# Layer norm, S4 convolution and NF4 gated MLP: the first weight tile's codes loaded in two halves, and another written order of the first tiles

## The chip, the cores and the metric

The kernel runs on one core of a Trainium2 chip. The metric is the device time of one execution in microseconds (us); lower is better. The engines that matter here are TensorE (PE, matrix products and transposes), VectorE (DVE), ScalarE (ACT), GpSimd (POOL) and SyncE (SP), which only issues DMAs. ACT issues a few DMAs too.

## The reference

For tokens x (2048 rows of 512 values, single precision) it computes, with xn the layer norm of x:

```python
x + s4(xn) + down(silu(gate(xn)) * up(xn))
```

`s4` is a causal convolution along the 512 features with a kernel derived from a state-space model. `gate` and `up` map 512 to 1792 features, and `down` maps back. Their weights are stored as 4-bit codes (one integer in 0..15 for each weight) and one scale for each block of 64 weights: weight = table[code] * scale, with a table of 16 values. Decoding the codes is part of the work.

## The kernel before

The tokens are worked on in four blocks of 512 rows (block 0 to 3), each of which has four groups of 128 rows. The 1792 hidden features are worked on in 14 weight tiles of 128, and tile m has a gate part and an up part of 128 x 512 values each. For every tile and block PE multiplies the tile's weights with the block's transposed, normalised tokens; ACT applies silu to the gate product, DVE multiplies it with the up product, and the result goes to device memory. After all tiles come the products with the down weights. In between lie the convolution and the work that prepares its kernel.

Decoding a tile takes eight `bends` (line 264): ACT passes over the codes in place with a piecewise linear function, the first one reading the integers. Bend j reads what bend j - 1 wrote. A multiply by the scales on DVE follows (`mul`), and then, for all products except the first ones, the weights and the tokens are split into three parts each (`split`, `part_of`), so that one product in full precision becomes three passes over faster operands. The exception is `native`: weight tile 0 on blocks 0 and 1 is multiplied unsplit, in full precision (line 469).

For a block of tokens the steps are: `stats` for each row group j (mean and variance, DVE), `scale` for a pair of row groups (1/sqrt by POOL), `norm` for each row group (DVE), `turn` for a pair of row groups (8 transposes on PE, with the pair number 0 or 1), then `copy` (ACT copies the transposes out, blocks 0 and 1) or `h`, `l`, `e` (the three parts).

The order of the start is written out by hand in the string `HEAD`. Each word is a step, and each engine executes its instructions in the order in which the words issue them; a loop at the end of the head ties every instruction of ACT, DVE, PE, POOL and SP to the one before it on the same engine. What an engine executes therefore follows from the words that concern it; a word of ACT moved past a word of DVE alone changes nothing. The numbers in the words are:

- `bend.m.j.k.h`: weight tile m, bend j, k = 0 gate or 1 up, h = half of the 512 columns. Without k and h: both parts whole.
- `mul.m.k.h`, `w.m.part` (split of tile m's weights, part 0 on ACT, 1 and 2 on DVE)
- `stats.b.j`, `scale.b.pair`, `norm.b.j`, `turn.b.pair`, `copy.b.pair`: block b
- `native.k.b.j.c`: gate or up, block b, row pair j, column pair c (two matrix products)
- `pass.k.m.b.part`: one of the three passes, four matrix products
- `silu.m.b`, `gated.m.b` (DVE, and then a store by SP), `awake.n` (n transposes whose result nobody reads)

The loads are issued before the list: gate's codes of tile 0 by ACT (line 573), then by SP the four row groups of block 0 as four DMAs (line 576), up's codes and the scales of tile 0, blocks 1 and 2, tile 1, block 3 and tile 2. The semaphores of these DMAs are used in rotation, eight of them, so each DMA from the ninth on waits for the landing of the one eight before it.

In the old list ACT has 19 bends of tile 0, then `copy.0.0`, two bends, `copy.0.1`, and the remaining eleven bends. PE has `awake.43`, `turn.0.0`, `awake.6`, `turn.0.1`, and then the native products. After the list an automatic scheduler orders the rest.

Of the kernel before, what the change touches and what calls it, by code (L numbers as in the profile page):

```python
# [9 lines left out]
I32 = mybir.dt.int32  # L10
# [8 lines left out]
HD = 512  # L19
# [44 lines left out]


HEAD = """
awake.43 stats.0.0 bend.0.0.0.0 bend.0.0.0.1 bend.0.1.0.0 stats.0.1 bend.0.1.0.1
bend.0.2.0.0 stats.0.2 bend.0.2.0.1 scale.0.0 bend.0.3.0.0 bend.0.3.0.1 stats.0.3
bend.0.4.0.0 bend.0.5.0.0 norm.0.0 bend.0.4.0.1 scale.0.1 bend.0.6.0.0 norm.0.1 bend.0.5.0.1
bend.0.7.0.0 turn.0.0 awake.6 bend.0.0.1.0 mul.0.0.0 bend.0.6.0.1 norm.0.3 bend.0.1.1.0  # L70
bend.0.7.0.1 norm.0.2 bend.0.2.1.0 mul.0.0.1 copy.0.0 turn.0.1 stats.1.0 bend.0.3.1.0
native.0.0.0.0 stats.1.1 bend.0.0.1.1 copy.0.1 native.0.0.0.1 stats.1.2 scale.1.0
bend.0.4.1.0 native.0.0.1.0 stats.1.3 bend.0.1.1.1 bend.0.5.1.0 bend.0.2.1.1 norm.1.1
native.0.0.1.1 scale.1.1 bend.0.6.1.0 norm.1.0 bend.0.7.1.0 bend.0.3.1.1 turn.1.0 mul.0.1.0
bend.0.4.1.1 norm.1.2 bend.0.5.1.1 native.1.0.0.0 norm.1.3 bend.0.6.1.1 bend.0.7.1.1
native.1.0.1.0 copy.1.0 mul.0.1.1 stats.2.1 turn.1.1 silu.0.0 stats.2.0 native.1.0.0.1 w.0.0
stats.2.3 scale.2.0 native.1.0.1.1 copy.1.1 stats.2.2 native.1.1.0.0 bend.1.0 norm.2.0
scale.2.1 native.1.1.0.1 norm.2.1 bend.1.1 gated.0.0 turn.2.0 norm.2.3 native.0.1.0.0 h.2.0
norm.2.2 w.0.1 turn.2.1 bend.1.2 native.0.1.0.1 e.2.0 bend.1.3 native.1.1.1.0 l.2.0 h.2.1
native.0.1.1.0 bend.1.4 native.0.1.1.1 e.2.1 native.1.1.1.1 bend.1.5 l.2.1 pass.0.0.2.0  # L80
bend.1.6 w.0.2 pass.1.0.2.0 bend.1.7 pass.0.0.2.1 stats.3.1 silu.0.1 pass.1.0.2.1 mul.1
load.3.0 bend.2.0 pass.0.0.2.2 stats.3.0 w.1.0 pass.1.0.2.2 gated.0.1 scale.3.0 bend.2.1
pass.0.1.2.0 w.1.1 h.0 pass.1.1.2.0 stats.3.2 pass.1.1.2.1 w.1.2 bend.2.2 pass.0.1.2.1
stats.3.3 pass.0.1.0.0 silu.0.2 bend.2.3 l.0 scale.3.1 pass.1.1.2.2 h.1 pass.0.1.2.2
pass.1.1.0.0 norm.3.0 e.0 bend.3.0 pass.1.1.0.1 pass.0.1.1.0 bend.2.4 pass.0.1.0.1 norm.3.3
silu.1.2 gated.0.2 pass.0.1.0.2 bend.3.1 norm.3.2 pass.1.1.0.2 norm.3.1 bend.3.2 gated.1.2
turn.3.1 silu.1.0 l.1 turn.3.0 pass.1.1.1.0 h.3.0 gated.1.0 pass.0.1.1.1 h.3.1 l.3.0
pass.1.1.1.1 bend.2.5 pass.0.1.3.0 l.3.1 bend.2.6 pass.1.1.3.0 e.3.0 bend.3.3 pass.0.1.3.1
e.3.1 bend.3.4 pass.0.0.3.0 pass.0.0.3.1 bend.2.7 e.1 pass.1.1.3.1 bend.3.5 pass.0.1.3.2
bend.3.6 mul.2 pass.0.0.3.2 bend.3.7 pass.1.0.3.0 mul.3 pass.1.1.3.2 pass.0.1.1.2 silu.1.3  # L90
w.2.0 pass.1.0.3.1 silu.0.3 w.2.1 pass.1.1.1.2 pass.0.2.0.0 silu.1.1 w.2.2 w.3.0
pass.1.2.0.0 w.3.1 pass.0.2.0.1 pass.1.2.0.1 gated.1.3 pass.1.2.0.2 gated.1.1 w.3.2
pass.0.2.0.2 pass.1.0.3.2 silu.2.0 gated.2.0 gated.0.3
"""


# [1 line left out]
def layernorm_s4_nf4_glu_kernel(  # L98
# [19 lines left out]
    V, S, G, T = nc.vector, nc.scalar, nc.gpsimd, nc.tensor  # L118
# [119 lines left out]
    def load_q(pair):  # L238
        n = "".join(f"{kind}{m}" for kind, m in pair)
        q = work.tile([P, 2, 512], F32, tag="q", name=f"q_{n}", bufs=3)  # L240
        sc = work.tile([P, 2, 512], F32, tag="sc", name=f"sc_{n}")
        qs[pair] = (q, sc, n)

    def load_codes(pair, k, eng):
        kind, m = pair[k]
        eng.dma_start(qs[pair][0][:, k, :].bitcast(I32), SRC[kind][0][m])
# [11 lines left out]
    def load_weights(pair):  # L258
        load_q(pair)
        for k in range(2):  # L260
            load_codes(pair, k, nc.sync)
            load_scales(pair, k)
# [256 lines left out]
        nc.sync.dma_start(res_dram[tb], xr)  # L519


    ALL = slice(0, HD)
    HALVES = (slice(0, HD // 2), slice(HD // 2, HD))

    def down(tb, wd):

        if tb == NTB - 1:
            po = [bank2(f"po{tb}_{j}")[:, 0, :] for j in range(4)]
        else:
            pj = [bank2(f"po{tb}_{jj}") for jj in range(2)]  # L530
            po = [pj[j // 2][:, j % 2, :] for j in range(4)]
        xr = work.tile([P, 4, HD], F32, tag="xt", name=f"xo{tb}")
        nc.gpsimd.dma_start(xr, res_dram[tb])  # L533
        for p in range(NPR):
            hr = work.tile([P, 2, 512], F32, tag="q", name=f"hr{tb}_{p}", bufs=3)
            nc.sync.dma_start(hr, h_dram[tb][p])
            hp = work.tile([P, 3, 2, 512], F32R, tag="wp", name=f"hp{tb}_{p}", bufs=4)
            split([hp[:, i, :, :] for i in range(3)], hr)
            for j in range(4):
                for k in range(2):  # L540
                    for part in range(3):
                        T.matmul(  # L542
                            po[j], hp[:, part, k, bass.ts(j, P)], wd(p, part, k),
                            start=(p == 0 and k == 0 and part == 0),
                            stop=(p == NPR - 1 and k == 1 and part == 2),
                        )
                if p == NPR - 1 and tb == NTB - 1:

                    for i, cs in enumerate(HALVES if j == 3 else (ALL,)):
                        o = xr[:, j, cs]  # L550
                        V.scalar_tensor_tensor(o, po[j][:, cs], OUT, o, ALU.mult, ALU.add)  # L551
                        (nc.scalar if i else nc.sync).dma_start(out[bass.ts(4 * tb + j, P), cs], o)
        if tb < NTB - 1:
            for jj in range(2):
                o = xr[:, 2 * jj : 2 * jj + 2, :]
                V.scalar_tensor_tensor(o, pj[jj], OUT, o, ALU.mult, ALU.add)
                nc.sync.dma_start(rows(out, tb)[:, 2 * jj : 2 * jj + 2, :], o)

    gu = lambda m: (("g", m), ("u", m))
# [9 lines left out]
    wp, ps, hs = {}, {}, {}  # L569
    sp = nc.sync  # L570
    load_q(gu(0))
    w0 = qs[gu(0)][0]
    load_codes(gu(0), 0, S)
    silu_set = const.tile([P, 1], F32, tag="silu_set", name="silu_set")
    S.activation(silu_set, mhalf[:, 0:1], AF.Silu)
    load_x(0, 1)
# [123 lines left out]
    for i in range((6 * NPR + 3) // 4):  # L700
        wt = work.tile([P, 4, 512], F32R, tag="xp", name=f"wdt{i}", bufs=12)
        s = 4 * i
        while s < min(4 * i + 4, 6 * NPR):
            e = min(4 * i + 4, 6 * (s // 6 + 1))
# [80 lines left out]
```

## Time and profile before

| what | us |
|---|---|
| median of three runs | 514.54 (514.51 to 515.04) |
| the profiled execution's own time | 514.13 |
| its span (first to last instruction) | 512.4 |
| PE busy | 507.1 (99% of the span) |
| DVE busy, ACT busy | 261.3, 264.3 |
| POOL busy | 24.5 |
| data moved by DMA | 96.33 MB, mean 188 GB/s |

Busy time is added up over the instructions of an engine. In the rows of a stage, the numbers stand for PE, PE's weight loads, DVE, ACT and POOL in this order, each followed by its number of instructions, and then the granted clock of PE, the mean busy share of the DMA engines, and the rate in GB/s. A row of the timeline or of the chain of waits begins with its start in the span and its length. "L267" is line 267 of the kernel before. In the trace each full-precision product of 256 columns makes two rows.

### The profile page before, as it was taken

The numbers are of one execution on the slowest core, as the hardware profiler recorded it, in microseconds if no ns is written. First come the engines' busy times: TensorE is split into PE (matmuls) and PEld (weight loads), VectorE is DVE, ScalarE is ACT, GpSimd is POOL, SyncE is SP. The second block draws the span as 40 slices with busy tenths as digits, with TensorE's granted clock in tenths as the row PEclk, the third lists the DMA queues.
The fourth block names the chain that finished last, engine by engine and source line by source line (L and its number), as shares of the span: only waits on it lengthen the run. The fifth ranks groups of instructions, "written<-read, shape, count | busy, mean of one in ns | idle before, by whom it ended". The sixth has DMA issues, their size and how long they took to land.

```text
span 512.4 us, 6160 instructions
## 1 busy us (share of the span) xinstructions
PE 507.1 (99%) x2345; PEld 425.4 (83%) x2345; DVE 261.3 (51%) x351; ACT 264.3 (52%) x335; POOL 24.5 (5%) x42
## 2 busy tenths in 40 slices
PE   8999999999999999999999999999999999999997
PEld 8888888888888888888888888888888888888885
DVE  6999789955436473433514313114536436437412
ACT  7998869799899987995262102012122121121100
POOL 2312002000000000000000000121000000000000
PEclk9999999999999999999999999999999999999999
DMA  8942254878765778663835222789633624624102
GB/s 305 306 134 106 75 172 146 279 245 308 280 210 184 276 273 293 225 204 125 302 129 205 104 82 83 295 308 349 208 112 135 217 100 148 219 87 157 50 0 82
DMA packets 37006, 96.33 MB, mean 188 GB/s; under 512 B 4592, under 2 KB 5360, under 8 KB 34160
## 3 DMA queue, kind: packets, MB, share of 16 engines
q1 hardware_dynamic: 34096, 80.34, 45.1%
q0 software_dynamic: 2592, 15.21, 8.3%
q8 instruction: 18, 0.29, 0.3%
q10 hardware_dynamic: 288, 0.39, 0.2%
q14 instruction: 12, 0.10, 0.1%
HBM read 61.84 MB, written 34.08 MB: 187 GB/s over the span
## 4 chain that ended last, share of the span: by engine, by line
PE 97%; ACT 1%; DMA 1%; DVE 0%; issue 0%; DVEq 0%
PE gu L461 57%; PE po L542 30%; PE pc L508 5%; PE gu L469 3%; PE pt L207 1%; ACT q_g0u L267 1%; DMA q_g0u<-in_gate_q_dram 1%; PE pc L513 1%; PE pm L433 0%; DVE x L195 0%; PE pss L358 0%; DVE xo L551 0%; DVEq L781 0%; DVE q_g0u L634 0%
## 5 line engine op out<-in xcount | busy, mean ns | idle before, releaser
L542 PE MATMUL po<-wdt,hp 128*128 128x512 f32 x672 | 152.5, 389 | 0.0
L542 PEld LDWEIGHTS po<-wdt,hp 128*128 128x128 f32 x672 | 126.1, 188 | 26.2
L481 DVE SCALAR_TENSOR_TENSOR h<-gu,h 128x512 f32<-128x512 f32 x56 | 38.4, 688 | 112.1 <-ACT h L477 112.0
L146 ACT ACTIVATE hp<-hr 128x1024 fp32r<-128x1024 f32 x28 | 29.7, 1060 | 104.7 <-PE po L542 100.7
L477 ACT ACTIVATE h<-gu 128x512 f32<-128x512 f32 x56 | 33.0, 590 | 91.0 <-PE gu L461 91.0
L148 DVE TENSOR_TENSOR hp<-hr,hp 128x1024 fp32r<-128x1024 f32 x28 | 34.3, 1226 | 62.7 <-ACT hp L146 62.7
L150 DVE SCALAR_TENSOR_TENSOR hp<-hp 128x1024 fp32r<-128x1024 f32 x28 | 34.3, 1224 | 1.0
L461 PE MATMUL gu<-xhT,wp_gu 128*128 128x512 f32 x112 | 29.7, 393 | 0.0
L461 PE MATMUL gu<-xlT,wp_gu 128*128 128x512 f32 x112 | 29.1, 389 | 0.0
L461 PE MATMUL gu<-xeT,wp_gu 128*128 128x512 f32 x112 | 28.8, 389 | 0.0
L461 PEld LDWEIGHTS gu<-xlT,wp_gu 128*128 128x128 f32 x112 | 21.0, 188 | 4.4
L461 PEld LDWEIGHTS gu<-xeT,wp_gu 128*128 128x128 f32 x112 | 21.0, 188 | 4.4
L461 PEld LDWEIGHTS gu<-xhT,wp_gu 128*128 128x128 f32 x112 | 20.9, 188 | 4.2
L508 PE MATMUL pc<-tp,xhT 128*128 128x512 f32 (+2 forms) x48 | 17.2, 358 | 0.0
L508 PE MATMUL pc<-tp,xeT 128*128 128x512 f32 (+2 forms) x48 | 16.3, 340 | 0.0
L508 PE MATMUL pc<-tp,xlT 128*128 128x512 f32 (+2 forms) x48 | 16.1, 336 | 0.0
L469 PE MATMUL gu<-xf,q_g0u 128*128 128x256 f32 x64 | 14.7, 381 | 0.0
L469 PEld LDWEIGHTS gu<-xf,q_g0u 128*128 128x128 f32 x64 | 11.8, 190 | 1.6 <-ACT xf L213 0.2
L533 POOL DMA_DIRECT2D xo<-rd x4 | 2.4, 592 | 222.2 <-DMA rd<-xr 112.2
L184 DVE BATCH_NORM_STATS2 st<-x 128x6 f32<-128x512 f32 x16 | 10.7, 672 | 3.3 <-DMA x<-in_x_dram 3.3
L518 DVE SCALAR_TENSOR_TENSOR xr<-pc,xr 128x1024 f32<-128x1024 f32 x8 | 9.8, 1220 | 4.9 <-PE pc L513 4.9
L705 POOL DMA_DIRECT2D wdt<-wdd x14 | 7.4, 530 | 94.0 <-PE gu L461 85.3
(272 smaller groups left out, 891.1 us busy)
## 6 DMA issues: line engine op xcount, KB each, us to landing
hd<-h SPq DMA_DIRECT2D x56, 256.0 KB, 2.7
hr<-hd SPq DMA_DIRECT2D x28, 512.0 KB, 3.3
wdt<-wdd POOLq DMA_DIRECT2D x7, 1024.0 KB, 8.2
xr<-in_x_dram SPq DMA_DIRECT2D x4, 1024.0 KB, 5.7
rd<-xr SPq DMA_DIRECT2D x4, 1024.0 KB, 4.4
xo<-rd POOLq DMA_DIRECT2D x4, 1024.0 KB, 6.2
wdt<-wdd POOLq DMA_DIRECT2D x7, 512.0 KB, 7.1
x<-in_x_dram SPq DMA_DIRECT2D x6, 512.0 KB, 6.1
```

Of the source, the lines that this page charges most:

```text
L146: S.activation(dst[0], src, AF.Copy, scale=TRIM)
L148: V.tensor_tensor(dst[1], src, f(dst[0]), ALU.subtract)
L150: V.scalar_tensor_tensor(dst[2], f(dst[1]), -LAM, f(dst[0]), ALU.mult, ALU.add)
L184: V.bn_stats(st[:, j, :], xs[tb][:, j, :])
L461: T.matmul(ps[:, k, :], wp[:, part, k, bass.ts(c, P)], xT[tb][part][:, :, c, :], start=(part == 0 and c == 0), stop=(part == 2 and c == NC ...
L469: T.matmul(ps[:, k, j.start * P : j.stop * P], w[:, k, bass.ts(c, P)], xf[tb].rearrange("p j (c q) -> p j c q", c=NC)[:, j, c, :], start=( ...
L477: S.activation(h, pg, AF.Silu, scale=unit)
L481: V.scalar_tensor_tensor(h, pu, unit, h, ALU.mult, ALU.mult)
L508: T.matmul(po[:, k, i * P : HD], xT[tb][part][:, jj + k, i, :], toep[:, part, 0 : HD - i * P], start=(i == 0 and part == 0), stop=False,)
L518: V.scalar_tensor_tensor(o, po, OUT, o, ALU.mult, ALU.add)
L542: T.matmul(po[j], hp[:, part, k, bass.ts(j, P)], wd(p, part, k), start=(p == 0 and k == 0 and part == 0), stop=(p == NPR - 1 and k == 1 an ...
L705: nc.gpsimd.dma_start(f(wt[:, s - 4 * i : e - 4 * i, :]), wd_dram[s // 6][:, s % 6 : s % 6 + e - s, :])
```

## The change

The first load is split. Gate's codes of tile 0, 128 rows of 512 integers, were one DMA on ACT's queue. Now columns 0 to 255 are the first DMA of SP's queue, and columns 256 to 511 a DMA on ACT's queue. SP issues the four row groups of block 0 after that, as before.

The list is replaced by another. On ACT, the bends of gate's second half now stand ahead of those of the first half, 20 bends instead of 19 come before `copy.0.0`, two more before `copy.0.1`, and ten after it. On DVE, `norm.0.2` and `norm.0.3` change places, so do `stats.1.0` and `stats.1.1`, and `norm.1.3` comes after `mul.0.1.1`. On PE, `native.1.0.0.1` now comes before `turn.1.1`, block 1's gate products are mixed with the up products of block 0, and `turn.2.1` comes before `turn.2.0`. On POOL, `scale.2.1` comes before `scale.2.0`. Further down the list the passes, splits and token blocks are mixed differently, and behind it the automatic scheduler places loads and stores on SP differently. The line numbers behind the list grow by one to four.

The diff, with the second half of both lists cut:

```diff
 HEAD = """
-awake.43 stats.0.0 bend.0.0.0.0 bend.0.0.0.1 bend.0.1.0.0 stats.0.1 bend.0.1.0.1
-bend.0.2.0.0 stats.0.2 bend.0.2.0.1 scale.0.0 bend.0.3.0.0 bend.0.3.0.1 stats.0.3
-bend.0.4.0.0 bend.0.5.0.0 norm.0.0 bend.0.4.0.1 scale.0.1 bend.0.6.0.0 norm.0.1 bend.0.5.0.1
-bend.0.7.0.0 turn.0.0 awake.6 bend.0.0.1.0 mul.0.0.0 bend.0.6.0.1 norm.0.3 bend.0.1.1.0
-bend.0.7.0.1 norm.0.2 bend.0.2.1.0 mul.0.0.1 copy.0.0 turn.0.1 stats.1.0 bend.0.3.1.0
-native.0.0.0.0 stats.1.1 bend.0.0.1.1 copy.0.1 native.0.0.0.1 stats.1.2 scale.1.0
-bend.0.4.1.0 native.0.0.1.0 stats.1.3 bend.0.1.1.1 bend.0.5.1.0 bend.0.2.1.1 norm.1.1
-native.0.0.1.1 scale.1.1 bend.0.6.1.0 norm.1.0 bend.0.7.1.0 bend.0.3.1.1 turn.1.0 mul.0.1.0
-bend.0.4.1.1 norm.1.2 bend.0.5.1.1 native.1.0.0.0 norm.1.3 bend.0.6.1.1 bend.0.7.1.1
-native.1.0.1.0 copy.1.0 mul.0.1.1 stats.2.1 turn.1.1 silu.0.0 stats.2.0 native.1.0.0.1 w.0.0
-stats.2.3 scale.2.0 native.1.0.1.1 copy.1.1 stats.2.2 native.1.1.0.0 bend.1.0 norm.2.0
-scale.2.1 native.1.1.0.1 norm.2.1 bend.1.1 gated.0.0 turn.2.0 norm.2.3 native.0.1.0.0 h.2.0
...
+bend.0.0.0.1 bend.0.0.0.0 bend.0.1.0.1 awake.43 stats.0.0 bend.0.1.0.0 bend.0.2.0.1
+stats.0.1 bend.0.2.0.0 bend.0.3.0.1 bend.0.3.0.0 stats.0.2 scale.0.0 bend.0.4.0.1
+bend.0.4.0.0 bend.0.5.0.1 stats.0.3 bend.0.5.0.0 bend.0.6.0.0 norm.0.0 scale.0.1
+bend.0.7.0.0 norm.0.1 bend.0.0.1.0 bend.0.6.0.1 mul.0.0.0 turn.0.0 awake.6 bend.0.1.1.0
+norm.0.2 bend.0.2.1.0 bend.0.7.0.1 norm.0.3 bend.0.3.1.0 mul.0.0.1 copy.0.0 turn.0.1
+stats.1.1 bend.0.0.1.1 native.0.0.0.0 stats.1.0 bend.0.4.1.0 copy.0.1 native.0.0.0.1
+stats.1.2 scale.1.0 bend.0.1.1.1 native.0.0.1.0 stats.1.3 bend.0.5.1.0 bend.0.6.1.0
+bend.0.2.1.1 norm.1.1 native.0.0.1.1 scale.1.1 bend.0.7.1.0 norm.1.0 bend.0.3.1.1 mul.0.1.0
+turn.1.0 bend.0.4.1.1 bend.0.5.1.1 norm.1.2 bend.0.6.1.1 native.1.0.0.0 bend.0.7.1.1
+copy.1.0 native.1.0.1.0 mul.0.1.1 norm.1.3 silu.0.0 native.1.0.0.1 stats.2.2 w.0.0 turn.1.1
+stats.2.3 stats.2.0 native.0.1.0.0 scale.2.1 copy.1.1 stats.2.1 native.1.0.1.1 bend.1.0
+norm.2.2 scale.2.0 native.0.1.1.0 gated.0.0 bend.1.1 native.0.1.0.1 norm.2.3 bend.1.2
...
 """
...
-    load_codes(gu(0), 0, S)
+
+    for eng, cs in zip((sp, S), HALVES):
+        eng.dma_start(w0[:, 0, cs].bitcast(I32), gate_q[0][:, cs])
```

`HALVES`, the column slices 0 to 255 and 256 to 511, existed already and is only defined earlier in the file.

More of the change, by code (lines that the diff above doesn't have):

```diff
@@ L79 @@
[L79 to L90, printed above, removed]
@@ L91 @@
-w.2.0 pass.1.0.3.1 silu.0.3 w.2.1 pass.1.1.1.2 pass.0.2.0.0 silu.1.1 w.2.2 w.3.0
-pass.1.2.0.0 w.3.1 pass.0.2.0.1 pass.1.2.0.1 gated.1.3 pass.1.2.0.2 gated.1.1 w.3.2
-pass.0.2.0.2 pass.1.0.3.2 silu.2.0 gated.2.0 gated.0.3
+bend.0.0.0.1 bend.0.0.0.0 bend.0.1.0.1 awake.43 stats.0.0 bend.0.1.0.0 bend.0.2.0.1
+stats.0.1 bend.0.2.0.0 bend.0.3.0.1 bend.0.3.0.0 stats.0.2 scale.0.0 bend.0.4.0.1
+bend.0.4.0.0 bend.0.5.0.1 stats.0.3 bend.0.5.0.0 bend.0.6.0.0 norm.0.0 scale.0.1
+bend.0.7.0.0 norm.0.1 bend.0.0.1.0 bend.0.6.0.1 mul.0.0.0 turn.0.0 awake.6 bend.0.1.1.0
@@ new lines @@
+stats.2.3 stats.2.0 native.0.1.0.0 scale.2.1 copy.1.1 stats.2.1 native.1.0.1.1 bend.1.0
+norm.2.2 scale.2.0 native.0.1.1.0 gated.0.0 bend.1.1 native.0.1.0.1 norm.2.3 bend.1.2
+norm.2.0 turn.2.1 norm.2.1 stats.3.0 bend.1.3 turn.2.0 w.0.1 native.1.1.0.0 h.2.0
+native.1.1.1.0 h.2.1 e.2.0 native.0.1.1.1 bend.1.4 l.2.0 native.1.1.0.1 silu.0.1
+native.1.1.1.1 l.2.1 bend.1.5 pass.0.0.2.0 bend.1.6 w.0.2 pass.0.0.2.1 bend.1.7 e.2.1
+pass.1.0.2.0 h.0 pass.1.0.2.1 mul.1 load.3.0 pass.0.0.2.2 stats.3.1 w.1.0 pass.1.0.2.2
@@ new lines @@
+gated.0.1 scale.3.0 bend.2.0 pass.0.1.0.0 w.1.1 pass.0.1.2.0 bend.2.1 l.0 pass.1.1.2.0
+bend.2.2 pass.1.1.0.0 bend.2.3 w.1.2 pass.0.1.2.1 bend.2.4 pass.1.1.2.1 stats.3.2 bend.3.0
+pass.0.1.2.2 norm.3.0 stats.3.3 h.1 pass.1.1.0.1 norm.3.1 scale.3.1 pass.1.1.2.2 e.0
+silu.0.2 pass.0.1.0.1 bend.3.1 turn.3.0 norm.3.2 silu.1.2 pass.0.1.0.2 norm.3.3 h.3.0
+gated.0.2 pass.1.1.0.2 gated.1.2 bend.3.2 turn.3.1 e.3.0 silu.1.0 pass.0.1.1.0 h.3.1
+gated.1.0 pass.1.1.1.0 l.3.0 bend.2.5 pass.0.1.3.0 bend.2.6 l.3.1 pass.0.0.3.0 bend.3.3
@@ L94 @@
+pass.1.1.3.0 e.1 pass.0.1.3.1 bend.2.7 pass.1.1.3.1 bend.3.4 e.3.1 pass.0.0.3.1 mul.2
+pass.1.0.3.0 pass.0.0.3.2 l.1 pass.1.0.3.1 silu.0.3 w.2.0 pass.1.0.3.2 bend.3.5 w.2.1
+pass.1.1.3.2 pass.0.1.3.2 bend.3.6 w.2.2 pass.0.2.0.0 silu.1.3 gated.0.3 bend.3.7
+pass.0.1.1.1 pass.1.2.0.0 mul.3 pass.1.2.0.1 pass.0.1.1.2 pass.1.1.1.1 pass.1.1.1.2
+pass.0.2.0.1 silu.1.1 w.3.0 gated.1.1 pass.1.2.0.2 w.3.1 pass.0.2.0.2 silu.2.0 gated.1.3
+w.3.2 gated.2.0
 """
@@ L242, in load_q @@
         qs[pair] = (q, sc, n)
+    ALL = slice(0, HD)
+    HALVES = (slice(0, HD // 2), slice(HD // 2, HD))
     def load_codes(pair, k, eng):
@@ L519, in conv @@
         nc.sync.dma_start(res_dram[tb], xr)
-    ALL = slice(0, HD)
-    HALVES = (slice(0, HD // 2), slice(HD // 2, HD))
     def down(tb, wd):
```

## The prediction

> **What bounds the kernel now.** I read the busy times by stage first. TensorE (PE) is busy for every microsecond from 10.44 to 500. Its columns below are the stage, its length, then busy time and instruction count of each engine.
>
> ```profile
> 10.44:30.00 19.56, 19.56 (x109) 17.33 (x110) 17.92 (x34) 18.73 (x36) 4.42 (x8) 1.00 0.81 271
> 30.00:90.00 60.00, 60.00 (x279) 49.99 (x278) 54.08 (x91) 51.28 (x74) 7.00 (x5) 1.00 0.41 130
> 90.00:500.00 410.00, 410.00 (x1866) 342.56 (x1865) 180.94 (x210) 186.86 (x208) 10.15 (x19) 1.00 0.55 193
> ```
>
> The table of waits agrees: PE waits twice in the whole execution, and both waits are over by 10.44.
>
> ```profile
> PE warm L591 <- POOL ident masks.py:199: 1.4, 1, 1.4
> PE pt L207 <- DVE x L195: 0.3, 1, 0.3
> ```
>
> So the span is the moment at which real products begin, plus a fixed stream of PE work, plus a short tail. The chain of waits tells what sets that moment (start, length, what).
>
> ```profile
> 0.79 3.65 DMA q_g0u<-in_gate_q_dram
> 4.44 0.02 issue
> 4.46 2.88 ACT q_g0u L267 x9
> 7.34 0.02 issue
> 7.37 1.65 ACT q_g0u L267 x5
> 9.02 0.02 issue
> 9.04 0.04 DVE q_g0u L634
> 9.08 0.31 issue
> 9.39 1.01 DVE x L195 x2
> 10.39 0.04 issue
> 10.44 1.09 PE pt L207 x8
> 11.53 3.68 PE gu L469 x16
> ```
>
> Gate's codes land at 4.44, ScalarE (ACT) bends them, and a multiply on VectorE (DVE) stands in front of the last two normalisations of token block 0. The timeline shows a second chain that ends at the same time: ACT's copy of the first transposes, which the first product reads.
>
> ```profile
> 10.45 0.99 ACT L213 COPY xf<-pt 128x1024 f32<-128x1024 f32 x1
> ...
> 11.49 3.72 PE L469 MATMUL gu<-xf,q_g0u 128*128 128x256 f32 x16
> ...
> 11.96 0.99 ACT L213 COPY xf<-pt 128x1024 f32<-128x1024 f32 x1
> ...
> 12.86 4.20 ACT L267 ACTIVATE q_g0u<-q_g0u 128x256 f32<-128x256 f32 x11
> ```
>
> The copy ends at 11.44, the transposes at 11.5. Whatever the change does, the first product starts at the later of the two, and that shift reaches the end of the span one for one unless PE later runs dry.
>
> **The halves.** The last view is that of the DMA issues (KB each, then us from issue to landing).
>
> ```profile
> q_g0u<-in_gate_q_dram ACTq DMA_DIRECT2D x1, 256.0 KB, 3.6
> q_g3u<-in_gate_q_dram SPq DMA_DIRECT2D x1, 256.0 KB, 2.7
> x<-in_x_dram SPq DMA_DIRECT2D x4, 256.0 KB, 3.8
> q_g0u<-in_up_q_dram SPq DMA_DIRECT2D x1, 256.0 KB, 4.7
> ```
>
> The first bend will wait for ACT's half and the second for SP's. Call the landing of the later one L. Lower bound: the same 256 KB on quiet engines, 2.7 us (q_g3u), so L = 3.5. Upper bound for a halving that gains nothing: 4.44. In between I count bytes. From 2 us on the engines move about 390 GB/s (the rates of the first 6 us), 0.67 us per 256 KB. Today gate's codes and the first token tile are issued together, share the engines, and have both landed by 4.44 (the first statistics start at 4.30). With the change the first token tile comes one SP issue later, behind SP's half. Until both halves are in, about 256 KB of codes and some 64 KB of tokens have moved, 192 KB less than 512, or 0.50 us: L = 3.95. I take it; it lies midway between the ends, and both ends stay in the range.
>
> The Trainium skill speaks against this part ("DMA: Bandwidth & Descriptors", section "Issuing engines are not separate DMA queues"): transfers started from several engines run on the same 16 DMA engines, and only issue time is saved. By that rule alone L would stay at 4.44, and the sum below would end 0.52 us above the one I take.
>
> **The order on ACT.** Before the first copy the new list has 20 bends, the old one 19. A bend that follows one of another half starts 0.31 us after it (nine bends in 2.88 with 0.40 for the last: 2.48/8). One that follows its own half waits for it: 7.37 - (4.46 + 8 x 0.31) = 0.43; the group of eleven (five such pairs among ten steps, 3.80 us) gives 0.45. The old order has one such pair before the copy: 18 x 0.31 + 0.43 = 6.0, measured 10.45 - 4.46 = 5.99. The new order runs gate's bends 5, 6, 7 of the first half in a row, and up's bends 1 and 2: three pairs, 17 x 0.307 + 3 x 0.44 = 6.54. So the order costs 0.55 us and gives back what the halves save. Copy: L + 0.02 + 6.54 = 10.51. The first product: 1.04 later as before (10.45 to 11.49), **11.55 instead of 11.49: +0.06 us**. With L = 3.5: -0.39; with 4.44: +0.55.
>
> **The tokens.** SP issues one more DMA ahead of the four token tiles (0.45 us each). Bytes ahead of the first tile are those that shared the engines with it anyway, so it lands 0 to 0.45 us later, and I take 0.2. Cover: its transposes need the second normalisation, over at 8.48, while PE is in its 43 warming transposes to 8.49 and only then turns the first tile: 0.4 us. The next pair: the second scale on GpSimd (POOL) ends at 9.05 + 0.2; the multiply needs 14 bends, 3.95 + 4.66, and ends its claim on DVE at 9.0. Normalisations at 9.28 and 9.74, second group of transposes at 10.33, over by 10.8 (today 11.5). The new order also puts them in the order in which PE reads them. The transposes are therefore no longer the last; a **new wait of PE of 0.6 us for ACT's copy** takes the place of the 0.3 us wait for DVE. The other loads queue in a stream that the engines' rate bounds: 0 to +0.1 us, and block 1's codes land about 3 us before ACT comes to them.
>
> **The rest of the list.** Nothing is added or removed on PE, DVE or POOL. Where the order puts something earlier, I added up its queue (first product at 11.55):
> - Up's product on chunk 2 of the first pair now goes ahead of block 1's second transposes. ACT: the second copy starts 1.52 after the first, then 0.90, then ten bends with five pairs (4 x 0.31 + 5 x 0.44 + 0.40): 16.8; multiply on DVE to 17.2. PE comes to it at 11.55 + 3.68 + 0.87 + 1.73 = 17.8. Cover 0.6.
> - Block 1's last normalisation now stands behind that multiply: 17.7. PE wants it at 18.7. Cover 1.0.
> - The first product of weight tile 1 on block 0. ACT, from the end of block 1's transposes at 19.8: copy 0.90, eight bends 4.16, two splits of block 2 1.82, eight bends 4.16, silu 0.48, split of block 0 1.81, split of the weights 1.06: 34.2. PE, from 19.6: 16 product rows of 0.216, two groups of transposes, 20 more rows, then six passes of 0.91: 34.5. Cover 0.3, the thinnest I find; the old order, added up this way, ends 0.2 us before the trace does. Price 0 to 0.5; I take 0, because both sums start at the same transposes.
> - POOL's two scales of block 2 change places (the normalisations that read them do too), and the stores of hidden activations and the later loads change places on SP; PE's waits name no DMA, and from 90 us on ACT and DVE are busy 187 and 181 of 410 us, so late feeding has slack. Bounds 0 and +0.3; I take 0.
>
> **Sum.** Profiled execution 514.13 us (span 512.4) + 0.06 = 514.19. It lies 0.41 under the median of the runs, 514.54; on the median the forecast is **514.6 us**. A difference of 0.2%, 1.03 us, is what a measurement of this kernel can tell from no change: the runs themselves reach from 514.51 to 515.04.
>
> **Rivals.**
> 1. The halves land as fast as a lone transfer, L = 3.5: -0.39, **514.1**. For it: they are first in both queues. Against it: they share the engines with each other's rows and with a token tile, and 1 KB rows come twice as many.
> 2. The halving gains nothing, L = 4.44, and the extra bend and two pairs are paid: +0.55, **515.1**. For it: the bytes and the engines are the same.
> 3. The other side: the half behind the other queue's rows lands like the transfers later in the queue (3.8 to 4.7 us after issue; up's codes, 4.7): L = 5.5, +1.6, **516.1**. It decides from L = 4.95 on, where the shift passes 1.03. Place: ACT's first or second bend. Against it: those rows had a megabyte in front of them, these have none.
> 4. PE runs dry in the products between 13 and 60 us because the thin cover fails and blocks behind it slip: from a delay of ACT of 1.3 us on it costs over 1 us, **515.7**. Against it: the covers above.
> 5. The change does not do what it says: both halves are needed by the second bend, so the split buys only position in the queue. That is rival 2.
> A gain over 0.6 us is shut out: warming to 8.49, 16 transposes (1.75) and the six in between (0.65) end at 10.9.
>
> **How the numbers follow.** Forecast (L from 3.75 to 4.2) 0.60; rival 1 0.14; rival 2 0.14; rival 3 0.06; rival 4 0.04; 0.02 for a cause that lowers the time and that I do not see. The first three are all within 0.2%: same 0.88; slower 0.10; faster 0.02. The range reaches from rival 1 (514.1, less 0.1 for the runs' scatter) to rival 2 with its thin cover (515.1 + 0.3): 514.0 to 515.4.
>
> **What the changed profile would show.** Right: ACT's first bend at about 3.95; the first copy at 10.5; PE waiting 0.5 to 0.7 us for that copy, none for DVE; first product at 11.4 to 11.7; PE full from there to 500. The halves' step is wrong if the first bend starts before 3.7 or after 4.2; the pairs' step if 20 bends take other than 6.5; the tokens' step if PE's wait names DVE; the covers if any PE wait stands after 12 us, at 34 us first of all.

## The result, and the profile after

The changed kernel is slower: 515.55 us, the median of 22 runs (514.31 to 517.88), against 514.19 (513.93 to 515.04) of 22 runs of the kernel before. The ratio is 1.0025, with a 95% interval from 1.0018 to 1.0031, that is 0.9 to 1.6 us. The forecast, 514.6 within 514.0 to 515.4, was too low. The runs of the new kernel also scatter over 3.6 us, those of the old one over 1.1.

The profiled execution took 515.61 us with a span of 513.9, which is 1.5 more than before. From 30.5 us on PE is full, as before. (Columns as in the first fence of the prediction.)

```profile
30.50:90.00 59.50, 59.50 (x276) 49.38 (x275) 53.03 (x99) 50.19 (x73) 4.05 (x5) 1.00 0.36 116
90.00:500.00 410.00, 410.00 (x1867) 342.55 (x1866) 183.96 (x201) 187.39 (x209) 12.93 (x20) 1.00 0.55 195
```

So the loss lies ahead of that. The table of waits of PE has a new line, and it is not a wait for ACT:

```profile
PE warm L594 <- POOL ident masks.py:199: 1.4, 1, 1.4
PE pt L208 <- issue: 0.9, 1, 0.9
PE pt L208 <- DVE x L196: 0.4, 1, 0.4
```

The chain of waits now runs over the token tiles instead of gate's codes (start, length, what). The lines with "SPq" are SP issuing its loads one after the other:

```profile
0.80 0.39 SPq L576
...
2.17 0.44 SPq L175
...
2.65 5.24 DMA x<-in_x_dram
...
7.92 0.70 DVE st L185
...
9.32 1.11 PE pt L208 x8
...
12.10 3.57 PE gu L473 x16
15.66 0.85 issue
16.52 1.06 PE pt L208 x8
```

The fourth token tile of block 0, issued at 2.65, lands at 7.89; before, it was issued at 2.17 and landed at 6.45. "issue" names no releaser: what PE waits for at 15.66 has to be read from the timeline, which shows who was held up by late loads:

```profile
3.68 4.69 ACT L271 ACTIVATE q_g0u<-q_g0u 128x256 f32<-128x256 int32 x14 [0.96 <-DMA q_g0u<-in_gate_q_dram]
...
5.92 0.69 DVE L185 BATCH_NORM_STATS2 st<-x 128x6 f32<-128x512 f32 x1 [0.75 <-DMA x<-in_x_dram]
...
8.89 2.10 ACT L271 ACTIVATE q_g0u<-q_g0u 128x256 f32<-128x256 int32 x6 [0.52 <-DMA q_g0u<-in_up_q_dram]
...
10.90 0.99 ACT L214 COPY xf<-pt 128x1024 f32<-128x1024 f32 x1
...
11.94 3.72 PE L473 MATMUL gu<-xf,q_g0u 128*128 128x256 f32 x16
...
12.23 0.69 DVE L185 BATCH_NORM_STATS2 st<-x 128x6 f32<-128x512 f32 x1 [0.51 <-DMA x<-in_x_dram]
...
15.44 0.97 DVE L196 TENSOR_SCALAR x<-x,mv,rstd 128x512 f32<-128x512 f32 x2
...
16.52 1.06 PE L208 MATMUL pt<-ident,x 128*128 128x128 f32 x8 [0.85 <-issue]
```

The same two normalisations of block 1 in the kernel before, where PE did not wait for them:

```profile
13.83 0.97 DVE L195 TENSOR_SCALAR x<-x,mv,rstd 128x512 f32<-128x512 f32 x2
```

Read from the top: the halves are there at 3.66, earlier than forecast, and ACT starts at 3.68. DVE gets the second token tile at 5.90 (before 4.96). ACT has done gate's 14 bends by 8.37 and then stands 0.52 for up's codes, which land at 8.87 (before 7.32). Its copy comes at 10.90, and the first product at 11.94 instead of 11.49. At 12.21 the first pair of block 1 lands (before 10.37), and PE, through with its first 16 product rows at 15.66, stands 0.85 for the tokens of block 1, whose normalisation ends at 16.41 (before 14.80). The sum: 0.45 at the first product, 0.85 for block 1, and 0.19 because the eight transposes after that stall take 1.06 instead of 0.87 in the chain. That is 1.49 of 1.5 us.

The loads themselves, from the DMA issues up to 16 us (KB each, then the median of us from issue to landing; before, the tokens' 256 KB took 3.8 and up's codes 4.7):

```profile
x<-in_x_dram SPq DMA_DIRECT2D x4, 256.0 KB, 4.5
q_g0u<-in_up_q_dram SPq DMA_DIRECT2D x1, 256.0 KB, 5.7
...
q_g0u<-in_gate_q_dram ACTq DMA_DIRECT2D x1, 128.0 KB, 2.9
q_g0u<-in_gate_q_dram SPq DMA_DIRECT2D x1, 128.0 KB, 2.7
```

Why they take longer is seen in the mean busy share of the 16 DMA engines from 3.2 to 5.2 us, one digit for each 0.05 us, in tenths. First the kernel before, then the changed one:

```profile
DMA  8969979999799896997998999959879499497996
```
```profile
DMA  8999969476365699996799536625445763994997
```

In the changed kernel the engines are partly empty from about 3.5 to 3.9, between the landing of the codes (3.49 and 3.66) and that of the first tile (its arrivals are at 3.82 to 4.24), and again from 4.3 to 4.9. The trace records 16 arrivals for every load. Sorted, those of the second token tile are:

```
before, issued 1.24:  4.63 4.64 4.65 4.67 4.68 4.69 4.71 4.72 4.73 4.75 4.76 4.78 4.79 4.80 4.83 4.96
after,  issued 1.71:  4.53 4.60 4.79 4.80 4.82 4.84 4.85 4.87 5.62 5.63 5.64 5.65 5.67 5.68 5.77 5.90
```

Half of the arrivals are as early as before, the other half comes 0.8 us later. At 4.23 to 4.29 the trace has seven packets of 2 KB that take 0.65 to 0.75 us each, and an eighth at 3.94 that takes 0.71, where most take 0.084: as many as there are late arrivals. The same number, or two more, stays behind in the third tile, the fourth, up's codes and the scales: once a part of the stream is late, every load behind it is late, since a load is there when its last part is. The Trainium skill describes this counting ("DMA: Bandwidth & Descriptors", section "Why a DMA increments its semaphore by 16 and not by 1"): a DMA runs on up to 16 engines that finish independently, and each adds one to the semaphore. The 16 arrivals, 4.53 to 5.90, agree with it. The rotation of the semaphores adds to the delay, since SP issues a load only when the one eight before it has landed: the second pair of block 1 goes out at 6.93, right after the third tile's landing at 6.91, and not at 6.26 as before.

### The profile page after: what moved, and what is told of

Same layout as the page of the kernel before. It is cut to its first block, busy times and chain, and to the rows that moved or that the text cites. A ratio compares the mean times of both kernels' runs of the same rounds, so it can differ in the third digit from the quotient of the medians.

```text
span 513.9 us, 6166 instructions
## 1 busy us (share of the span) xinstructions
PE 507.7 (99%) x2345; PEld 425.4 (83%) x2345; DVE 262.3 (51%) x351; ACT 263.6 (51%) x335; POOL 24.5 (5%) x42
## 4 chain that ended last, share of the span: by engine, by line
PE 97%; DMA 1%; DVE 0%; SPq 0%; issue 0%; DVEq 0%
PE gu L465 57%; PE po L543 30%; PE pc L512 5%; PE gu L473 3%; PE pt L208 1%; DMA x<-in_x_dram 1%; PE pc L517 1%; PE pm L437 0%; SPq L175 0%; PE pss L362 0%; DVE st L185 0%; PE warm L594 0%; DVE x L196 0%; DVE xo L552 0%; SPq L576 0%
## 5 line engine op out<-in xcount | busy, mean ns | idle before, releaser
L271 ACT ACTIVATE q_g0u<-q_g0u 128x256 f32<-128x256 f32 (+1 forms) x32 | 11.1, 407 | 1.7 <-DMA q_g0u<-in_gate_q_dram 1.0
```

What stands on the lines that cost most here:

```text
L271: S.activation(w, w if j else w.bitcast(I32), AF.Prelu, scale=scale, bias=bias, alpha=slope)
```

## The experiments

Letters in the quoted expectations: A looks for the cause in the loads, B in the list. A1 and D blame the short rows of 1 KB, A2 the codes' place ahead of the tokens. C lets the late issue of the tokens empty the engines, C1 by the lateness alone, C2 only together with a short queue on ACT. E (late) and F (behind another load) belong to the last three runs. All ratios are against the kernel before, run on the same chip, with 95% intervals; they follow the means of the runs more closely than the medians. The table gives SP's issue and the landing of the last token tile of block 0 in each kernel's profile; "excess" is by how much its landing moved more than its issue, both against the kernel before (2.17 and 6.45). The first product is read from the timeline. These readings are of one execution each, whose own time is given beside the median: those of the repetition, of "whole, small load first" and of "token tile first" are the slowest of their kernels, so their landings stand for a bad case and not for the median. The kernel with the tokens in pairs is not in the table, since it has no such tile.

| kernel | issue | landing | excess | first product | this execution, us | median us | ratio |
|---|---|---|---|---|---|---|---|
| kernel before | 2.17 | 6.45 | 0 | 11.49 | 514.13 | 514.17 to 514.30 | 1 |
| changed kernel | 2.65 | 7.89 | 0.96 | 11.94 | 515.61 | 515.55 | 1.0025 |
| the same again | 2.65 | 8.27 | 1.34 | 12.98 | 516.57 | 515.59 | 1.0021 |
| halves, old list | 2.65 | 7.47 | 0.54 | 12.12 | 515.45 | 515.91 | 1.0026 |
| new list, load whole | 2.18 | 6.27 | -0.19 | 11.92 | 514.61 | 514.75 | 1.0011 |
| halves by rows | 2.98 | 8.29 | 1.03 | 12.57 | 515.94 | 515.87 | 1.0033 |
| both halves on ACT | 2.17 | 6.80 | 0.35 | 12.61 | 515.30 | 515.26 | 1.0019 |
| whole, small load first | 2.65 | 9.52 | 2.59 | 15.06 | 517.52 | 516.11 | 1.0039 |
| tile 2 on ACT | 2.18 | 6.34 | -0.12 | 11.44 | 514.54 | 514.65 | 1.0007 |
| tile 2 on ACT, old list | 2.18 | 6.38 | -0.08 | 11.69 | 514.25 | 514.45 | 1.0005 |
| kernel before, small load first | 2.65 | 8.55 | 1.62 | 13.13 | 516.07 | 516.07 | 1.0031 |
| up's codes on ACT | 2.65 | 8.08 | 1.15 | 12.40 | 515.50 | 515.07 | 1.0014 |
| token tile first | 2.18 | 7.15 | 0.69 | 11.69 | 514.89 | 514.47 | 1.0000 |
| small load second | 2.65 | 6.89 | -0.04 | 11.41 | 514.59 | 514.72 | 1.0011 |
| first tile held back | 3.13 | 7.35 | -0.06 | 12.61 | 515.24 | 515.57 | 1.0027 |
| held back twice as long | 3.71 | 8.12 | 0.13 | 13.36 | 516.04 | 516.15 | 1.0037 |

**The two parts apart.** The kernel before with the halves only:

```diff
-    load_codes(gu(0), 0, S)
+    for eng, cs in zip((sp, S), HALVES):
+        eng.dma_start(w0[:, 0, cs].bitcast(I32), gate_q[0][:, cs])
```

> The old list with the new loads. In the profile of the changed kernel the codes landed at 3.66, and the token tiles of block 0 landed at 4.2, 5.9, 6.9 and 7.9 us instead of 4.3, 5.0, 5.7 and 6.4. Theory A, the column halves disturb the loads behind them whatever the list: the same late tiles here, last one at 7.5 to 8.2, the first product later than 11.5, the time 0.5 to 2 us over the kernel before. Theory B, the list is at fault and the loads were late by chance: tiles as before, the first product 0 to 0.4 us earlier, time equal to or up to 0.4 us under the kernel before.

Measured: 515.91 (514.24 to 516.60), ratio 1.0026 (1.0016 to 1.0036), the whole loss. The halves landed at 3.64, the token tiles at 4.21, 6.00, 6.64 and 7.47, and PE waited in the same places, for DVE (here twice) and at block 1's tokens:

```profile
PE pt L207 <- DVE x L195: 0.7, 2, 0.4
PE pt L207 <- issue: 0.6, 1, 0.6
```

The changed kernel with the first load whole again (the diff of above in reverse, the new list kept):

> The new list with the old loads (gate's codes whole on ACT's queue). Theory A: tiles land as before (last at 6.4); ACT begins at 4.46, its 20 bends with three pairs take 6.5 and the first product starts at 12.0, so the time is 0.4 to 0.6 us over the kernel before, and its runs scatter as little as those of the kernel before. Theory B: PE also runs dry later in the list, time 1 us or more over the kernel before with a PE wait behind 13 us.

Measured: 514.75 (514.52 to 515.69), ratio 1.0011 (1.0003 to 1.0020), +0.52 us. Tokens land as before, and only ACT's copy is late. First the wait of PE, then the chain of waits:

```profile
PE gu L473 <- ACT xf L214: 0.8, 1, 0.8
```
```profile
0.79 3.48 DMA q_g0u<-in_gate_q_dram
4.30 3.80 ACT q_g0u L271 x12
...
10.96 0.91 ACT xf L214
11.92 3.72 PE gu L473 x16
```

So the load is the cause of the loss and the list is not. The list alone costs about half a microsecond, on ACT, and this half does not add to the loss of the load: together they cost no more than the load alone.

**Chance, and rows of 1 KB.** The changed kernel a second time, with no edit, and then with the halves taken by rows (64 rows of 2 KB each instead of 128 of 1 KB):

```diff
-    for eng, cs in zip((sp, S), HALVES):
-        eng.dma_start(w0[:, 0, cs].bitcast(I32), gate_q[0][:, cs])
+    for eng, ps_ in zip((sp, S), (slice(0, 64), slice(64, P))):
+        eng.dma_start(w0[ps_, 0, :].bitcast(I32), gate_q[0][ps_, :])
```

> The changed kernel once more, for a second trace. If the late token tiles belong to the change, they are late again (last one at 7.2 to 8.5, block 1's first pair at 11.5 to 12.5) and the time is 0.8 to 2 us over the kernel before. If they were an accident of one execution, the last tile lands at 6.4 to 6.8 and the first product starts at 11.0 to 11.3, with a time 0.2 to 0.4 us under the kernel before.

> The changed kernel with the halves cut by rows: 64 rows of 2 KB on each queue instead of 128 rows of 1 KB. Theory A1, the short rows are what disturbs: tiles land as in the kernel before (last at 6.4 to 6.8), first product at 11.1 to 11.5, time 0 to 0.4 us under the kernel before. Theory A2, it is the place in the queue (codes on both queues ahead of the tokens): last tile at 7.5 to 8.2 as in the changed kernel, time 0.5 to 2 us over the kernel before.

Measured: the repetition 515.59, ratio 1.0021 (1.0013 to 1.0030); by rows 515.87, ratio 1.0033 (1.0021 to 1.0046). The loss is there each time, but not in the same place: in the repetition 2 of the 16 arrivals are late, by 1.0 to 1.8 us from the second tile to up's codes, and by rows one of them, by 1.0 to 1.5, from the third tile on. The short rows are not the cause. That the late ones are eight, two or one, and late by different amounts, may be where the scatter of the runs comes from; this was not followed further.

**Does the lateness of the tokens suffice?** Both halves on ACT's queue, so that SP begins with the tokens again; and the whole load on ACT with a small load (64 bytes of each of 128 rows, read by nobody) ahead of the tokens on SP:

```diff
-    for eng, cs in zip((sp, S), HALVES):
+    for eng, cs in zip((S, S), HALVES):
```
```diff
-    for eng, cs in zip((sp, S), HALVES):
-        eng.dma_start(w0[:, 0, cs].bitcast(I32), gate_q[0][:, cs])
+    load_codes(gu(0), 0, S)
+    fill = const.tile([P, 16], F32, tag="fill2", name="fill2")
+    sp.dma_start(fill, x[0:P, 0:16])
```

> The changed kernel with both column halves on ACT's queue, so that SP starts with the tokens as before. Theory C: the first token tile and the codes are through by 3.5, the next tile's descriptors are not there yet, some DMA engines stand empty at 3.6 to 4.0 and take up to 1 us to start again, and every later load waits for the slowest engine. Then with 256 KB on ACT's queue again the engines stay covered: no gap at 3.6 to 4.0, last tile of block 0 at 6.3 to 6.7, ACT's first bend at 4.2 to 4.5, the time as with the new list and the whole load, 514.6 to 515.0. Theory D, rows of 1 KB are the cause: gap and late tiles (last at 7.4 or later), 515.3 or more.

> The new list with gate's codes whole on ACT's queue, and on SP a load of 128 rows of 64 bytes (into a tile that nobody reads) ahead of the tokens: the tokens are issued as late as in the changed kernel, but ACT's queue keeps its 256 KB. Theory C1, lateness of the token issues alone empties the engines: gap at 3.6 to 4.0, last tile at 7.4 or later, 515.3 or more. Theory C2, it takes the short queue on ACT as well: no gap, last tile at 6.5 to 6.9, 514.6 to 515.1.

Measured: both halves on ACT 515.26, ratio 1.0019 (1.0011 to 1.0028), above what was expected. No gap of the engines at 3.6, but the later half, issued at 1.22, landed only at 4.96. The new list begins with it, so ACT's first bend came at 4.99 instead of the expected 4.2 to 4.5, and with its 20 bends PE waited for the copy as in the experiment with the whole load (0.8 us, first product 12.61, 1.12 later than before): this loss is ACT's. And yet 2 of the 16 arrivals fall behind here too, by 0.4 to 0.9 us from the third tile on, though SP's queue begins with the tokens; the last tile came at 6.80, after the expected 6.3 to 6.7. With the small load: 516.11, ratio 1.0039 (1.0027 to 1.0051), the largest ratio of all, although gate's codes landed at 3.62. The chain (of the slowest of its six runs, 517.52) shows one token tile that took 6.46 us, because one of its 16 arrivals is 2.4 us behind the others:

```profile
2.18 6.46 DMA x<-in_x_dram
```

Eight kilobytes ahead of the tokens are enough; neither the halves nor a short queue on ACT is needed.

The same small load in the kernel before, with nothing else changed, was made to see whether the old list is hit as well:

```diff
+    fill = const.tile([P, 16], F32, tag="fill2", name="fill2")
+    sp.dma_start(fill, x[0:P, 0:16])
     load_x(0, 1)
```

> The kernel before, with one edit: SP first loads 128 rows of 64 bytes into a tile that nobody reads, so the tokens are issued 0.45 us later; gate's codes stay whole on ACT's queue, the list is the old one. Theory C1, a second token tile that is issued at 1.71 instead of 1.24 comes too late for engines that are through with the first: engines stand empty between 3.6 and 4.3, the last tile of block 0 lands at 7.4 or later, and the time is 0.8 to 2 us over the kernel before. Rival, the new list or the halves are needed for the loss: last tile at 6.5 to 6.9, time 0 to 0.5 us over.

Measured: 516.07 (515.48 to 516.65), ratio 1.0031 (1.0019 to 1.0043). The share of the DMA engines from 3.2 to 5.2 us has such a hole too, and the issues show the small load itself and what is late:

```profile
DMA  9999999997164684576957959999548659587496
```
```profile
x<-in_x_dram SPq DMA_DIRECT2D x4, 256.0 KB, 4.9
q_g0u<-in_gate_q_dram ACTq DMA_DIRECT2D x1, 256.0 KB, 2.7
q_g0u<-in_up_q_dram SPq DMA_DIRECT2D x1, 256.0 KB, 6.6
fill<-in_x_dram SPq DMA_DIRECT2D x1, 8.0 KB, 2.4
```

Gate's codes are there 0.94 us earlier than before (3.50 against 4.44) and it helps nothing; up's codes, at 9.71, hold ACT for 1.66.

**Taking the lateness away.** The changed kernel with the second token tile on ACT's queue behind its half, so that two tiles are issued at 1.23 and 1.24:

```diff
+    xs[0] = work.tile([P, 4, HD], F32, tag="xt", name="x0", bufs=2)
+    for eng, j in ((sp, 0), (S, 1), (sp, 2), (sp, 3)):
+        eng.dma_start(xs[0][:, j : j + 1, :], rows(x, 0)[:, j : j + 1, :])
...
-    load_x(0, 1)
```

> The changed kernel with the second token tile on ACT's queue behind its half; SP has its half and tiles 1, 3 and 4. Theory C: both queues have work until 4 us, so no engine stands empty, tiles land at 4.2 to 4.6 and the last at 6.2 to 6.6; ACT begins at 3.7 and its copy sets the first product at 11.2 to 11.4: 513.8 to 514.2. Theory A2, the codes ahead of the tokens are the cause wherever the tokens are queued: last tile at 7.4 or later, 515.3 or more.

> The same loads with the old list. Theory C: tiles as in the run with the new list; 19 bends instead of 20 and one pair, so the copy is ready at 9.7 and the transposes set the first product at 11.0 to 11.2: 513.6 to 514.0. Theory A2: as there, 515.3 or more.

Measured: 514.65, ratio 1.0007 (0.9998 to 1.0015), with the new list; 514.45, ratio 1.0005 (0.9996 to 1.0014), with the old one. The hole is gone (share of the DMA engines, 3.2 to 5.2 us, new list), and what is left of the loss cannot be told from nothing:

```profile
DMA  9887999997999899899899996999979999999497
```

The gain that was expected of it did not come. With the new list the copy is at 10.22, where the forecast's sum puts it for a landing of 3.61, but the second group of transposes is over only at 11.6. With the old list:

```profile
9.51 1.01 ACT L213 COPY xf<-pt 128x1024 f32<-128x1024 f32 x1
...
10.76 1.09 PE L207 MATMUL pt<-ident,x 128*128 128x128 f32 x8 [0.63 <-DVE x L195]
...
11.69 1.68 PE L472 MATMUL gu<-xf,q_g0u 128*128 128x256 f32 x7
```

The copy comes 0.94 us earlier than before and waits for nothing; PE waits for the normalisation of the tokens, since the first tile, now behind a half of the codes, landed at 4.55 (before 4.28). What the codes gain the tokens lose, and in the kernel before both chains end within 0.1 us of each other: 11.44 and 11.5.

**Other orders of the same loads.** Up's codes on ACT's queue behind its half; a token tile first on SP, the halves on both queues around it, the second tile on ACT (old list; `tile_` loads a token tile, `half` a half of the codes); the tokens as two loads of 512 KB behind the half:

```diff
-    load_codes(gu(0), 1, sp)
+    load_codes(gu(0), 1, S)
```
```diff
...
+    tile_(sp, 0)
+    half(S, HALVES[0])
+    half(sp, HALVES[1])
+    tile_(S, 1)
+    tile_(sp, 2)
+    tile_(sp, 3)
...
```
```diff
-    load_x(0, 1)
+    load_x(0, 2)
```

> The changed kernel with up's codes (256 KB) moved from SP's queue to ACT's, right behind the half there; the token tiles are issued as late as in the changed kernel. If it is the standing empty that costs (an engine that runs out takes up to 1 us to start again), the other queue's work covers it: no gap at 3.6 to 4.0, last tile at 6.9 to 7.3 because 256 KB more go ahead of it, time 514.6 to 515.2. If the late issue hurts the tiles even with the engines at work, last tile at 7.8 or later and 515.4 or more.

> An attempt to be better than both, old list: SP issues token tile 1, gate's second half, tiles 3 and 4; ACT issues gate's first half and token tile 2. Theory C: no gap, first tile at 4.0 to 4.3, codes at 3.7 to 4.1, last tile at 6.2 to 6.5, first product at 11.0 to 11.4, 513.7 to 514.2. If what sets the start is how many bytes stand ahead of the statistics' tiles, it ends within 0.1 us of the kernel before.

> The changed kernel with block 0's tokens as two DMAs of 512 KB instead of four of 256: all tokens stay on SP's queue behind its half, but the rows of the second tile are issued at 1.24 with those of the first. Theory C1: no gap, the two pairs land at 4.9 to 5.1 and 6.2 to 6.5; the statistics start 0.7 later than with single tiles, the time is 514.6 to 515.2. If the one queue is the cause and not the time of issue: gap, last pair at 7.4 or later, 515.4 or more.

Measured: up's codes on ACT 515.07, ratio 1.0014 (1.0006 to 1.0023): less loss, no hole at 3.6, but 3 of the 16 arrivals fall behind by 0.4 to 0.9 us from the third tile on (three packets at 5.0 take 0.36 to 0.61 us; ACT's queue is through at 5.00), and the last tile lands at 8.08. The time is that of the first side of the expectation, the landing that of the second. Token tile first: 514.47, ratio 1.0000 (0.9992 to 1.0009), no better than the kernel before. In its slowest run, the profiled one, about half the engines were empty at 5.1 to 5.3, and the last tile landed at 7.15. Token pairs: 515.42, ratio 1.0022 (1.0012 to 1.0032), the time that the second expectation names; the last pair at 6.89, between the two; no hole at 3.6, and yet five packets of 0.63 to 0.72 us at 4.3 and a third of the arrivals 0.5 us behind. An empty stream at 3.6 is thus not needed for the loss.

**Late, or behind another load?** In all the kernels above that lost over 0.6 us, but for both halves on ACT, a load stands in front of the tokens, and the tokens are issued late; the next three were to part these. The small load behind the first tile:

```diff
-    load_x(0, 1)
...
+    for j in range(4):
+        if j == 1:
+            sp.dma_start(fill, x[0:P, 0:16])
+        nc.sync.dma_start(xs[0][:, j : j + 1, :], rows(x, 0)[:, j : j + 1, :])
```

> The kernel before with the small load (64 bytes a row, read by nobody) on SP's queue between the first and the second token tile, so that the first tile is issued at 0.80 as before and tiles 2 to 4 at 1.71, 2.17 and 2.65. Theory E, the DMA engines run out of work because the tokens are issued late: codes and first tile are 512 KB in hand until about 4.3, nothing runs dry; last tile of block 0 between 6.4 and 6.9, 514.1 to 514.8. Theory F, a further load in front of the tiles makes the engines pause, and the lateness does not matter: tile 2 is now third in its queue; last tile from 7.3 on, 515.2 to 516.5.

Measured: 514.72, ratio 1.0011 (1.0002 to 1.0020), last tile at 6.89. Tiles 2 to 4 are issued as late as in the changed kernel, behind an additional load, and land 0.2 to 0.5 us later than before; the last has an excess of -0.04. E's numbers hold, F's do not: with the first tile out at 0.80, a load in front of the other tiles cost 0.42 us and not 1 to 2.

The first tile held back by a fill of zeros that its load overwrites (320 columns, then twice 415; the four loads are written out behind it):

```diff
+    xs[0] = work.tile([P, 4, HD], F32, tag="xt", name="x0", bufs=2)
+    V.memset(xs[0][:, 0, 0:320], 0.0)
...
```

> The kernel before with the first token tile's load held back by a fill of zeros on VectorE (320 of the tile's 512 columns, about 0.35 us, overwritten by the load), so that SP issues it at about 1.2 instead of 0.80, with no further load. Theory E: as with the small load in front, some engines empty between 3.6 and 4, last tile of block 0 from 7.2 on, 515.3 to 516.5. Theory F: the queue has what it had before, every tile at most 0.45 later, last tile 6.4 to 6.9, 514.1 to 514.8.

> The same with the fill doubled and more (twice 415 columns, about 0.9 us), first token tile issued at about 1.7. Theory E: more engines empty and for longer, last tile at least 0.4 later than with the single fill, 515.7 to 517. Theory F: at most 0.9 later than before, last tile up to 7.35, 514.6 to 515.2.

Measured: 515.57, ratio 1.0027 (1.0017 to 1.0038), and 516.15, ratio 1.0037 (1.0024 to 1.0049). The edit did not do what was meant. The automatic scheduler put other loads into the gap, two (68 and 33 KB) and three (2 KB more) of them, and the first tile went out at 1.71 and 2.17, not at 1.24 and 1.7. The timeline of the first of the two:

```profile
0.80 0.39 SPq L294 DMA_DIRECT2D cols<-in_s_cols_dram  x1
...
1.24 0.42 SPq L295 DMA_DIRECT2D row<-in_s_row_dram  x1
1.71 1.85 SPq L579 DMA_DIRECT2D x<-in_x_dram  x4
```

So they do not tell late from behind, and this rival stays open. What they do show is that a stream with holes need not bring an excess: in the second the engines stand empty from 4.0 to 4.15 and have holes from 3.5 on (share from 3.2 to 5.2 us below), and yet the last tile is late by little more than its issue is (excess -0.06 and 0.13).

```profile
DMA  9997862319709855000119913565429589799898
```

**What is settled and what is open.** Settled: the loss comes from what stands ahead of the token tiles in SP's queue. One DMA ahead of the first tile, of 128 KB or of 8, with all tiles on that queue, put the median 0.9 to 1.9 us over the kernel before, in seven kernels with either list; the 8 KB behind the first tile brought 0.42; with one tile on the other queue 0.24 and 0.44 were left, which these runs cannot tell from nothing. Both halves on ACT lost 1.05 in another place, at ACT's copy. The delay of the tokens has two parts. The lateness of the issue, 0.48 us in most of these kernels, comes through one for one where it stands alone (small load second). The excess, 0.5 to 2.6 us in the profiled executions, comes with arrivals, one to ten of 16, that fall behind the others by 0.4 to 2.4 us and stay behind in the loads that follow.

Open is why they fall behind. Single packets that take 0.6 to 1.1 us between 3.9 and 4.5 are as many as the late arrivals of the second tile (for pairs, the second pair) in four kernels: eight in the changed one, seven with the old list, five with the token pairs, one with the small load first. In the others the counts differ, and four such packets (0.60 to 0.63 us, at 3.7 to 3.8) brought hardly any excess in the kernel held back twice as long. The trace does not tell which engine carried a packet. Holes in the stream do not decide it either: they come with the excess in the changed kernel, but there was none at 3.6 with the token pairs, and an almost entirely empty stream brought 0.13.

## Why the prediction was wrong

**The tokens: the step that failed.** It said "0 to 0.45 us later" for the first tile and took 0.2 for the rest; it said of the other loads that they "queue in a stream that the engines' rate bounds: 0 to +0.1 us". The first tile landed at 4.24, even before the old 4.28: right in effect. But the stream was not bound by the rate: the last tile came 1.45 later, up's codes 1.55, block 1's first pair 1.84. Of the covers that the step names, the 0.4 us for the first transposes was used up (the second tile came 0.94 later, and PE stood 0.42 for DVE at 9.32), and the "about 3 us" for block 1's codes was the wrong one to look at. The late loads that counted were up's codes (ACT stood 0.52) and block 1's tokens (PE stood 0.85), and the text priced neither. The step took a full stream for granted from a kernel in which the engines have work throughout these microseconds; what a later issue of the tokens does to that stream was not asked. Why a part of the stream then falls behind stays open.

**The halves.** L was taken as 3.95 with 3.5 as the lower end; the later half landed at 3.66. The mechanism was right, the size off by 0.3, and the first bend at 3.68 lies just ahead of the 3.7 that the text gave as a sign. The Trainium skill says ("DMA: Bandwidth & Descriptors", section "Issuing engines are not separate DMA queues") that issuing from several engines only saves the sequencer's issue time, which is usually small relative to the DMA. As to the issue time this agrees with the runs; its worth was larger here: giving one token tile to ACT's queue saves SP 0.47 us and took the time from 515.55 to 514.65. The 0.52 us that the prediction names for this rule (by its own terms 0.49, that is 0.55 less 0.06) concern the codes, and the codes did not set the end.

**The order on ACT.** 0.55 us and 6.54 us for 20 bends: right. With the load whole, first bend to copy took 6.57 (4.30 to 10.87) and the kernel lost 0.52; with tile 2 on ACT's queue 6.59 (3.63 to 10.22). In the changed kernel itself it took 7.22 (3.68 to 10.90), of which ACT stood 0.52 for up's codes.

**The new wait of PE.** Forecast 0.5 to 0.7 us for ACT's copy and none for DVE. Measured 0.4 for DVE and none for the copy: as the text said beforehand, a wait that names DVE means that the tokens' step is wrong. The wait for ACT's copy is there (0.8) in the two kernels with the new list and SP's tokens first: load whole, and both halves on ACT.

**The covers.** Those of the list (0.6 at up's product, 1.0 at block 1's last normalisation, 0.3 at 34 us) held: PE waits nowhere after 16.52 us. The wait at 15.66 is a PE wait after 12 us, which the text gave as the sign of a failed cover; but it is none of these covers, because it is a load that is late and not the list.

**The sum and the rivals.** 0.06 forecast, 1.36 measured between the medians. The codes' landing of 3.66 in the prediction's own sum gives a first product at 11.26 and 514.3, between the forecast and rival 1; the price found is near that of rivals 3 and 4 (516.1 and 515.7), but the mechanism is in neither. Rival 3 let the half be late, and the half was early. Rival 4 had PE run dry for lack of ACT's work, and it ran dry for lack of tokens. Missing was a rival for what is moved back in SP's queue, though the text counted that move.

## What to carry to other kernels

At the start of a kernel, when few bytes have been issued, a small DMA ahead of the large loads can cost more than its 0.45 us of issue, here up to 1.9 us in the median: look at the share of the DMA engines in fine slices after the first transfers land, and at the landing of the last load, not only of the first. If a load has to go in front, put it behind the first large one (0.42 us here), or give one of the large loads to the other queue. And before a chain is shortened, look whether a second one ends at the same moment and shares its resource: here codes that were 0.8 us earlier gained nothing in any run, since the tokens paid for it.

## What the runs showed that was not expected

- 8 KB ahead of the tokens cost 1.9 us (516.07 against 514.17), no less than the 128 KB of the half, 1.36 (the intervals overlap); the same 8 KB one place later cost 0.42.
- Seven 2 KB packets of 0.65 to 0.75 us at nearly the same moment, next to others of 0.084 us, in a stream that was half empty.
- A few late arrivals make all loads late for the next 6 us: the second tile's 0.94 is 1.84 at the first pair of block 1, which was issued 4.4 us later (about 0.5 of each is the later issue).
